# Cross-attention with a gate: score and weight transposes on VectorE, an earlier softmax, and another order of the attention products

## The chip, the cores and the metric

One core of a Trainium2 chip runs the kernel. The time is device microseconds of one execution, median of three runs; less is better. PE is TensorE's matmul row, PEld its weight loads, DVE is VectorE, ACT is ScalarE, POOL is GpSimd, SP issues most of the DMAs.

## What is computed

Everything is float32. Eight batches of 1024 tokens with 1024 features attend to 64 memory rows of 512 features each.

```python
memory_proj = jnp.einsum('bme,de->bmd', memory, W_mem)
scores = jnp.einsum('bnd,bmd->bnm', hidden_states, memory_proj) / jnp.sqrt(jnp.float32(D))
attn = jax.nn.softmax(scores, axis=-1)
memory_context = jnp.einsum('bnm,bmd->bnd', attn, memory_proj)
gate_input = jnp.concatenate([hidden_states, memory_context], axis=-1)
gate = jax.nn.sigmoid(jnp.einsum('bnf,df->bnd', gate_input, W_gate) + b_gate)
fused = hidden_states + gate * memory_context
return _rmsnorm(fused, norm_w)
```

## The kernel before

The tokens are worked on in 16 quads of 512 (four tiles of 128, `t` = 0 to 3). After a setup that multiplies the memory rows by both weight matrices, the large product of a quad is x times the first half of `W_gate`. It is done by Strassen's scheme in two levels: seven outer blocks a quad, in the order 1, 6, 7, 5, 4, 2, 3, and seven inner products each. An inner product is two matmuls over K in the program, four records on PE, and is called a **slot**: 49 slots a quad, slot 0 being the first product of block 1.

`outer_product` issues one block. Its products write four PSUM banks: `af` (its first half by R11 at the block's first slot, its second half by R22 at the sixth, its first half again by R21 at the seventh), `b` (kB, second slot), `c` (kC, third), and `ed` (fourth and fifth). Banks `af` and `ed` come in two sets that alternate by block; `b` and `c` are used again in every block. ACT copies the first half of `af` to `p1` (L901). DVE adds: `u2` = p1 + kB, `u3` = u2 + kC, `u4` = u2 + half of `ed`. POOL adds u3 and u4 to blocks of the output tiles `gate` (`pre`), DVE adds the whole banks (`fin_ed`, `fin_af`), and POOL also makes the left operands of the next block (`inner_s`, tile `l`).

After kC of blocks 4 and 3 come the **visits** (`visit`, L820), the products of the attention weights with the projected memory: for block 5 with 4, and for block 2 with 3. A visit puts the context into its own bank `pc` from rows 0 to 63 of the weights, and the gate's share of the memory into `af` or `ed` from rows 64 to 127, in 64x64 pieces. Before, the earlier block (5 or 2) goes first, with banks `b` and `c` as its `pc`; its sums are held back until then.

The order is written by hand. `plan` puts each step into the list of a slot (`at`), or beside a block (`mid`); `step` runs the list of a slot before its product is issued, in the order in which the entries were put there. The engines keep that program order: each has one queue. The steps that matter here, with t0 the quad's first slot:

- Scores of the next quad run on PE right after the visits of block 3 (`scores`, banks `af` and `ed` of the set that block 2 has just left); ACT copies, DVE adds (`add_scores`, slot 46). They come out with memory rows on partitions (`sT`).
- `transpose_scores` (slot 9) turns them on PE; `softmax_a` (slot 10) takes the maximum on DVE and four exponentials on ACT; `softmax_b` (slot 13) scales; `transpose_attn` (slot 18) turns them back on PE, and four ACT copies lay them out as `attnT`; `attn_difference` follows at slot 22. The visits are at slots 30 and 44.
- `square` of the quad before: tiles 2 and 3 at slots 3 and 4, tiles 0 and 1 at slots 22 and 23; the second of each pair ends with a Sqrt on ACT. `norm` multiplies on DVE and stores; for tiles 2 and 3 at slots 8, 10, 15 and 17, the first beginning with a reciprocal of the Sqrt's result.
- `outer_s` (sums of x blocks, DVE) at slots 3 and 11; `transpose_x` of the next quad at slots 20, 21, 23, 25, 37, 38, 42 and beside block 3.
- `gate` puts a sigmoid on ACT and, a slot or two later, the product with `pc` on DVE (`gated`).

Of the kernel before, what the change touches and what calls it, by code (L numbers as in the profile page):

```python
# [15 lines left out]
P = 128  # L16
# [4 lines left out]
def tile_gated_cross_attention_rmsnorm(  # L21
# [53 lines left out]
    NPAIR = BM // P  # L75
    SCALE = 1.0 / float(D) ** 0.5
    Q4 = D // 4

    const = ctx.enter_context(tc.tile_pool(name="const", bufs=1))
    gpool = ctx.enter_context(tc.tile_pool(name="gpool", bufs=7))  # L80
# [10 lines left out]
    def mm(o, lhsT, rhs, start, stop):  # L91
        pin(nc.tensor.matmul(o, lhsT, rhs, start=start, stop=stop, skip_group_check=True))  # L92

    def tt(eng, o, a, b, op):
        pin(eng.tensor_tensor(o, a, b, op))  # L95
# [4 lines left out]
    def t4k(pool, shape, tag, name):  # L100
        return pool.tile(shape, F32, tag=tag, name=name)
# [234 lines left out]


    A, S, L2, O = {}, {}, {}, {}
    sTs, attns, attnTs, scs, dens, mps, mgs = {}, {}, {}, {}, {}, {}, {}
    def where(q, t=0):  # L340
        return q // QPB, (q % QPB) * QT + t * P

# [79 lines left out]
        tt(nc.vector, flat, flat, part, ALU.add)  # L422
        sTs[q] = sT

    def transpose_scores(q):
        sc = ps_ctx.tile([P, 4, M], F32, tag="ctx", name=f"sc{q}")
        sT = sTs.pop(q)
        for t in range(2):
            pin(
                nc.tensor.transpose(  # L430
                    sc[:, 2 * t : 2 * t + 2, :].rearrange("p r m -> p (r m)"), sT[:, t, :], ident
                )
            )
        scs[q] = sc

    def softmax_a(q):
        sc = scs.pop(q)
        mx = t4k(small, [P, 4], "mx", f"mx{q}")
        pin(nc.vector.tensor_reduce(mx, sc, AX.X, ALU.max))
        pin(nc.scalar.activation(mx, mx, AF.Copy, scale=-SCALE))  # L440
        e = attns[q] = t4k(small, [P, 4, M], "e", f"e{q}")
        den = dens[q] = t4k(small, [P, 4], "den", f"den{q}")
        for t in range(4):
            pin(
                nc.scalar.activation(
                    e[:, t], sc[:, t], AF.Exp, bias=mx[:, t : t + 1], scale=SCALE, accum_out=den[:, t : t + 1]
                )
            )

    def softmax_b(q):  # L450
        e, den = attns[q], dens.pop(q)
        pin(nc.vector.reciprocal(den, den))
        for t in range(4):
            pin(nc.scalar.activation(e[:, t], e[:, t], AF.Copy, scale=den[:, t : t + 1]))

    def transpose_attn(q):
        attn = attns.pop(q)
        pa = ps_ctx.tile([P, 2, P], F32, tag="ctx", name=f"pa{q}")
        for t in range(2):
            pin(  # L460
                nc.tensor.transpose(  # L461
                    pa[:, t, :],
                    attn[:, 2 * t : 2 * t + 2, :].rearrange("p r m -> p (r m)"),
                    ident,
                )
            )

        at = attnTs[q] = t4k(small, [P, 8, P], "attnT", f"attnT{q}")
        for g in (1, 0):
            for r in range(2):  # L470
                pin(
                    nc.scalar.copy(
                        at[g * M : (g + 1) * M, 2 * r : 2 * r + 2, :], pa[r * M : (r + 1) * M]
                    )
                )

    def attn_difference(q):
        at = attnTs[q]
        tt(nc.vector, at[M:P, 4:6, :], at[M:P, 0:2, :], at[M:P, 2:4, :], ALU.subtract)
        tt(nc.vector, at[M:P, 6:8, :], at[M:P, 2:6:2, :], at[M:P, 3:6:2, :], ALU.subtract)  # L480

    def load_mp(b):
        mps[b] = t4k(small, [P, KD, M], "mpb", f"mpb{b}")
# [142 lines left out]
    def plan(q):  # L626
        t0 = SLOTS * q
        nxt = q + 1 < NQ
        for i, o in enumerate(ORDER):
            for part, t in ((0, 1), (1, 2)):  # L630
                if i + 1 < len(ORDER):
                    at(t0 + 7 * i + t, inner_s, q, ORDER[i + 1], part)
                elif nxt:
                    at(t0 + 7 * i + t, inner_s, q + 1, ORDER[0], part)
        if q == 0:
            at(t0 + 7, scores, q)
            at(t0 + 8, add_scores, q)
# [179 lines left out]
    sets = 0  # L817
    held = {}

    def visit(q, o, pcs, af, ed):  # L820

        row, h, g = EXT[o]
        at_, mg = attnTs[q], mgs[q // QPB]
        second = o in SECOND
        for r, k in ((0, af), (1, ed)):
            cols = slice(h * H, (h + 1) * H)
            for t in TOKENS:
                mm(pcs[r][t, :], at_[0:M, 2 * row + r, t], mg[0:M, cols], True, True)
            if second and r == 0:
                for n, left in ((0, g + r), (1, NEG[o])):  # L830
                    part = mg[M:P, h * H + n * C : h * H + (n + 1) * C]
                    for t in TOKENS:
                        mm(k[t, n], at_[M:P, left, t], part, False, True)
            else:
                whole = k.rearrange("p n c -> p (n c)")
                for t in TOKENS:
                    mm(whole[t, :], at_[M:P, g + r, t], mg[M:P, cols], second, True)

    def pre(q, o, u3, u4):

# [39 lines left out]
    def outer_product(q, o):  # L880
# [146 lines left out]
```

## Time and profile before

| | |
|---|---|
| median of three runs | 953.83 us (953.53 to 953.95) |
| the profiled execution's span | 951.8 us |
| PE busy | 939.9 us, 99% |
| DVE busy | 806.5 us, 85% |
| POOL busy | 711.0 us, 75% |
| ACT busy | 361.9 us, 38% |
| granted TensorE clock, mean | 0.997 |

How to read the lines that follow. A row of a timeline has the start in microseconds from the span's start, the duration, the engine, the line of the kernel, the operation, what it writes and reads with the shape, and how many were merged; in brackets the idle time before it and what ended that. A line can be a helper's: all matmuls are at L92, all sums of two tensors at L95. A row of a group has total busy time, mean nanoseconds of one, and idle time before. Matmuls are pipelined: the end of one is modelled, and the next starts before it; what a product takes is read from one start to the next.

### The profile page before, as it was taken

How to read it: one execution, taken by the hardware profiler on the slowest of the kernel's cores; microseconds unless marked ns; L12 is line 12 of the kernel's file. 1: busy time of each engine (PE TensorE's matmuls, PEld its weight loads, DVE VectorE, ACT ScalarE, POOL GpSimd, SP SyncE). 2: the span in 40 equal slices, each digit the busy share in tenths (PEclk: the TensorE clock that was granted, in tenths of full speed). 3: DMA queues.
4: the chain of work that ended last, by engine and by line, in shares of the span. 5: the costliest groups of instructions: out<-in, count | busy, mean ns of one | idle time of the engine just before them, and what ended most of it. 6: DMA issues, size and time to landing. Idle time of an engine off the chain costs nothing.

```text
span 951.8 us, 15584 instructions
## 1 busy us (share of the span) xinstructions
PE 939.9 (99%) x5624; PEld 732.1 (77%) x5624; DVE 806.5 (85%) x1258; ACT 361.9 (38%) x782; POOL 711.0 (75%) x780
## 2 busy tenths in 40 slices
PE   9999999999999999999999999999999999999995
PEld 8546778787877778787877778687877778787773
DVE  6988888888888888888888888888888888888887
ACT  3001235162433525153443526253443526243456
POOL 5997877688676777787686867777686767877683
PEclk9999999999999999999999999999999999999998
DMA  9956664482919365481918366391918466390632
GB/s 377 285 144 161 105 122 112 108 181 48 206 46 185 98 130 131 103 185 39 217 45 174 93 141 138 90 199 32 215 53 166 101 133 144 79 210 25 144 142 89
DMA packets 70923, 128.40 MB, mean 135 GB/s; under 512 B 12352, under 2 KB 49216, under 8 KB 70592
## 3 DMA queue, kind: packets, MB, share of 16 engines
q1 hardware_dynamic: 61664, 93.86, 37.5%
q0 software_dynamic: 9184, 33.56, 19.4%
q8 instruction: 45, 0.74, 0.3%
q14 instruction: 30, 0.25, 0.1%
HBM read 87.56 MB, written 41.68 MB: 136 GB/s over the span
## 4 chain that ended last, share of the span: by engine, by line
PE 97%; DVE 2%; ACT 1%; issue 0%; DVEq 0%
PE af L92 31%; PE ed L92 21%; PE pc L92 10%; PE kC L92 10%; PE kB L92 10%; PE pg L92 5%; PE psT_af L92 5%; PE pm L92 3%; DVE gate L95 1%; PE psT_ed L92 0%; PE pz L92 0%; DVE gate L788 0%; PE sc L430 0%; PE pa L461 0%; PE psT_b L92 0%; PE pt L193 0%
## 5 line engine op out<-in xcount | busy, mean ns | idle before, releaser
L95 POOL TENSOR_TENSOR gate<-gate,u 128x512 f32<-128x512 f32 (+1 forms) x224 | 236.9, 1070 | 187.4 <-DVE u L95 151.3
L685 ACT ACTIVATE gate<-gate 128x512 f32<-128x512 f32 x128 | 80.2, 630 | 225.0 <-DVE gate L95 225.0
L352 DVE STREAM_TRANSPOSE a<-xq 128x512 f32<-128x512 f32 x128 | 141.5, 1108 | 3.4 <-issue 3.4
L95 POOL TENSOR_TENSOR l<-a 128x256 f32<-128x256 f32 x128 | 110.9, 866 | 18.6 <-PE af L92 17.5
L714 DVE SCALAR_TENSOR_TENSOR gate<-gate,ss,nw_sb 128x512 f32<-128x512 f32 x120 | 119.4, 995 | 1.1
L92 PE MATMUL pc<-mg,attnT 64*64 64x512 f32 x512 | 116.8, 595 | 0.1
L92 PE MATMUL ed<-it,l 128*128 128x256 f32 x448 | 115.0, 379 | 0.0
L92 PE MATMUL kB<-it,l 128*128 128x256 f32 x448 | 115.0, 379 | 0.0
L95 DVE TENSOR_TENSOR gate<-gate,pc 128x512 f32<-128x512 f32 x128 | 86.1, 682 | 31.7 <-ACT gate L685 31.7
L901 ACT COPY u<-af 128x256 f32<-128x256 f32 x112 | 40.7, 363 | 182.6 <-PE af L92 182.6
L92 PE MATMUL af<-w,a 128*128 128x256 f32 x384 | 98.5, 379 | 0.0
L92 PEld LDWEIGHTS kB<-it,l 128*128 128x128 f32 x448 | 85.1, 190 | 11.6
L95 DVE TENSOR_TENSOR gate<-gate,ed 128x512 f32<-128x512 f32 x112 | 76.1, 679 | 19.1 <-POOL gate L95 17.5
L92 PEld LDWEIGHTS ed<-it,l 128*128 128x128 f32 x448 | 83.9, 190 | 10.7
L95 DVE TENSOR_TENSOR gate<-gate,af 128x512 f32<-128x512 f32 (+1 forms) x128 | 76.7, 609 | 12.8 <-PE af L92 11.2
L92 PEld LDWEIGHTS af<-w,a 128*128 128x128 f32 x384 | 73.0, 190 | 10.3 <-issue 0.5
L95 POOL TENSOR_TENSOR l<-s 128x256 f32<-128x256 f32 x96 | 78.2, 814 | 3.3 <-DVE it L95 3.3
L92 PEld LDWEIGHTS pc<-mg,attnT 64*64 64x64 f32 x512 | 32.9, 132 | 50.1 <-issue 23.5
L92 PE MATMUL af<-mg,attnT 64*64 64x256 f32 (+1 forms) x384 | 67.4, 456 | 0.0
L92 PE MATMUL ed<-it,a 128*128 128x256 f32 x256 | 67.4, 386 | 0.0
L95 DVE TENSOR_TENSOR u<-u,kC 128x256 f32<-128x256 f32 x112 | 45.9, 410 | 23.8 <-PE kC L92 20.3
L92 PE MATMUL af<-t,s 128*128 128x256 f32 x256 | 65.8, 379 | 0.0
(147 smaller groups left out, 2044.6 us busy)
## 6 DMA issues: line engine op xcount, KB each, us to landing
xq<-in_x SPq DMA_DIRECT2D x64, 512.0 KB, 10.3
gate<-in_x POOLq DMA_DIRECT2D x60, 512.0 KB, 8.4
out<-gate SPq DMA_DIRECT2D x60, 512.0 KB, 3.3
w<-in_w_gate_t SPq DMA_DIRECT2D x8, 512.0 KB, 10.2
w<-in_w_gate_t SPq DMA_DIRECT2D x2, 2048.0 KB, 17.2
mg<-mgd SPq DMA_DIRECT2D x16, 256.0 KB, 5.2
wm<-in_w_mem_t SPq DMA_DIRECT2D x4, 512.0 KB, 6.0
mpd<-mpT SPq DMA_DIRECT2D x4, 512.0 KB, 8.6
```

The source lines that it names most:

```text
L92: pin(nc.tensor.matmul(o, lhsT, rhs, start=start, stop=stop, skip_group_check=True))
L95: pin(eng.tensor_tensor(o, a, b, op))
L352: nc.vector.transpose(A[key][:, :, r * P : (r + 1) * P], chunks(xq[q][:, 4 * t : 4 * t + 4, :], KD)[:, half * KH : (half + 1) * KH],)
L685: pin(nc.scalar.activation(g, g, AF.Sigmoid))
L714: nc.vector.scalar_tensor_tensor(g[:, cols], g[:, cols], rstd[:, t % 2 : t % 2 + 1], nw_sb[:, cols], ALU.mult, ALU.mult,)
L901: pin(nc.scalar.copy(p1, af[:, 0]))
```

## The change

Four things are changed.

1. `turn_scores` and `turn_attn` turn scores and weights on DVE, in blocks of 32x32, where PE did it. With such blocks a token's 64 scores lie on two groups of 32 partitions, so the maximum and the sum of a token are each joined from two halves: `other_half` copies the other group's numbers over with four small ACT copies. There are eight exponentials and eight scalings of 32 columns, in two parts of four, where there were four and four of 64. `attnT` is filled by one DVE transpose and two ACT copies, its upper half in another order (`upper`).
2. The softmax's slots. From quad 1 on: turn and maximum at slot 0, exponentials at 3 and 9, scalings at 13 and 16, turning back at 19, differences at 22. In quad 0: 9, 11, 16, 19, 23, 25, 27.
3. The visits: later block's first half, the earlier block's two halves, later block's second half.
4. One x transpose moves from slot 42 to behind `u3` of block 3, ahead of the earlier block's sums.

```diff
+    def turn_scores(q):
+        sT = sTs.pop(q)
+        sc = scs[q] = t4k(small, [P, 2 * P // B32, B32], "sc", f"sc{q}")
+        pin(nc.vector.transpose(sc.rearrange("p n m -> p (n m)"), sT.rearrange("p t c -> p (t c)")))
+        mx = mxs[q] = t4k(small, [P, 2, 8], "mx", f"mx{q}")
+        pin(nc.vector.tensor_reduce(mx[:, 0], sc, AX.X, ALU.max))
+    def other_half(o, i):
+        for g in range(4):
+            pin(nc.scalar.copy(o[g * B32 : (g + 1) * B32], i[(g ^ 1) * B32 : ((g ^ 1) + 1) * B32]))
+    def softmax_max(q):
+        mx = mxs[q]
+        other_half(mx[:, 1], mx[:, 0])
+    def softmax_exp(q, part):
+        sc, mx = scs[q], mxs[q]
+        if part == 0:
+            dens[q] = t4k(small, [P, 2, 8], "den", f"den{q}")
+            tt(nc.vector, mx[:, 0], mx[:, 0], mx[:, 1], ALU.max)
+            pin(nc.scalar.activation(mx[:, 0], mx[:, 0], AF.Copy, scale=-SCALE))
+        for n in range(4 * part, 4 * part + 4):
             pin(
                 nc.scalar.activation(
...
+                    bias=mx[:, 0, n : n + 1],
+                    scale=SCALE,
+                    accum_out=dens[q][:, 0, n : n + 1],
                 )
             )
+        if part == 1:
+            del mxs[q]
+            other_half(dens[q][:, 1], dens[q][:, 0])
+    def softmax_scale(q, part):
+        sc, den = scs[q], dens[q]
+        if part == 0:
+            tt(nc.vector, den[:, 0], den[:, 0], den[:, 1], ALU.add)
+            pin(nc.vector.reciprocal(den[:, 0], den[:, 0]))
+        for n in range(4 * part, 4 * part + 4):
+            pin(nc.scalar.activation(sc[:, n], sc[:, n], AF.Copy, scale=den[:, 0, n : n + 1]))
+    def turn_attn(q):
+        sc = scs.pop(q)
+        at = attnTs[q] = t4k(small, [P, 8, P], "attnT", f"attnT{q}")
+        pin(
+            nc.vector.transpose(
+                at[:, 0:2].rearrange("p t c -> p (t c)"), sc.rearrange("p n m -> p (n m)")
+            )
+        )
+        for g in (1, 0):
             pin(
+                nc.scalar.copy(
+                    at[g * M : (g + 1) * M, 2:4, :], at[(1 - g) * M : (2 - g) * M, 0:2, :]
                 )
             )
...
-        at(t0 + 9, transpose_scores, q)
-        at(t0 + 10, softmax_a, q)
-        at(t0 + 13, softmax_b, q)
-        at(t0 + 18, transpose_attn, q)
-        at(t0 + 22, attn_difference, q)
+        when = (9, 11, 16, 19, 23, 25, 27) if q == 0 else (0, 3, 9, 13, 16, 19, 22)
+        at(t0 + when[0], turn_scores, q)
+        at(t0 + when[0], softmax_max, q)
+        for part in range(2):
+            at(t0 + when[1 + part], softmax_exp, q, part)
+            at(t0 + when[3 + part], softmax_scale, q, part)
+        at(t0 + when[5], turn_attn, q)
+        at(t0 + when[6], attn_difference, q)
...
-            (20, 0, 0), (21, 1, 0), (23, 2, 0), (25, 3, 0), (37, 2, 1), (38, 3, 1), (42, 0, 1)
+            (20, 0, 0), (21, 1, 0), (23, 2, 0), (25, 3, 0), (37, 2, 1), (38, 3, 1)
         ):
             at(t0 + i, transpose_x, q + 1, t, half)
+        mid((q, 3, 0), transpose_x, q + 1, 0, 1)
...
-            visit(q, f, fp, faf, fed)
             pcs = [ps_ctx.tile([P, H], F32, tag="ctx", name=f"pc{q}_{o}_{r}") for r in range(2)]
-            visit(q, o, pcs, af, ed)
+            visit(q, o, 0, pcs[0], af)
+            visit(q, f, 0, fp[0], faf)
+            visit(q, f, 1, fp[1], fed)
+            visit(q, o, 1, pcs[1], ed)
```

More of the change, by code (lines that the diff above doesn't have):

```diff
@@ L77, in tile_gated_cross_attention_rmsnorm @@
     Q4 = D // 4
+    B32 = 32
     const = ctx.enter_context(tc.tile_pool(name="const", bufs=1))
@@ L338, in tile_gated_cross_attention_rmsnorm @@
     A, S, L2, O = {}, {}, {}, {}
-    sTs, attns, attnTs, scs, dens, mps, mgs = {}, {}, {}, {}, {}, {}, {}
+    sTs, attnTs, scs, mxs, dens, mps, mgs = {}, {}, {}, {}, {}, {}, {}
     def where(q, t=0):
@@ L423, in add_scores @@
         sTs[q] = sT
-    def transpose_scores(q):
-        sc = ps_ctx.tile([P, 4, M], F32, tag="ctx", name=f"sc{q}")
+    def turn_scores(q):
         sT = sTs.pop(q)
-        for t in range(2):
-            pin(
-                nc.tensor.transpose(
-                    sc[:, 2 * t : 2 * t + 2, :].rearrange("p r m -> p (r m)"), sT[:, t, :], ident
-                )
-            )
-        scs[q] = sc
-    def softmax_a(q):
-        sc = scs.pop(q)
[L438 to L443, printed above, removed]
-            pin(
-                nc.scalar.activation(
-                    e[:, t], sc[:, t], AF.Exp, bias=mx[:, t : t + 1], scale=SCALE, accum_out=den[:, t : t + 1]
-                )
-            )
@@ L450, in softmax_b @@
[L450 to L475, printed above, removed]
+        sc = scs[q] = t4k(small, [P, 2 * P // B32, B32], "sc", f"sc{q}")
@@ new lines, in turn_scores @@
+        pin(nc.vector.transpose(sc.rearrange("p n m -> p (n m)"), sT.rearrange("p t c -> p (t c)")))
[14 more added lines that the diff above has]
+        for n in range(4 * part, 4 * part + 4):
+            pin(
+                nc.scalar.activation(
+                    sc[:, n],
+                    sc[:, n],
+                    AF.Exp,
+                    bias=mx[:, 0, n : n + 1],
+                    scale=SCALE,
+                    accum_out=dens[q][:, 0, n : n + 1],
+                )
+            )
+        if part == 1:
+            del mxs[q]
+            other_half(dens[q][:, 1], dens[q][:, 0])
@@ L477, in attn_difference, with upper @@
+    def upper(left):
+        return left ^ 2 if left < 4 else left
     def attn_difference(q):
         at = attnTs[q]
-        tt(nc.vector, at[M:P, 4:6, :], at[M:P, 0:2, :], at[M:P, 2:4, :], ALU.subtract)
-        tt(nc.vector, at[M:P, 6:8, :], at[M:P, 2:6:2, :], at[M:P, 3:6:2, :], ALU.subtract)
+        tt(nc.vector, at[M:P, 4:6, :], at[M:P, 2:4, :], at[M:P, 0:2, :], ALU.subtract)
+        tt(nc.vector, at[M:P, 6:8, :], at[M:P, 0:5:4, :], at[M:P, 1:6:4, :], ALU.subtract)
     def load_mp(b):
@@ L818, in tile_gated_cross_attention_rmsnorm, with visit @@
     held = {}
-    def visit(q, o, pcs, af, ed):
+    def visit(q, o, r, pc, k):
         row, h, g = EXT[o]
@@ L824, in visit @@
         second = o in SECOND
-        for r, k in ((0, af), (1, ed)):
-            cols = slice(h * H, (h + 1) * H)
-            for t in TOKENS:
[L828 to L837, printed above, removed]
+        cols = slice(h * H, (h + 1) * H)
+        for t in TOKENS:
+            mm(pc[t, :], at_[0:M, 2 * row + r, t], mg[0:M, cols], True, True)
+        if second and r == 0:
+            for n, left in ((0, g + r), (1, NEG[o])):
+                part = mg[M:P, h * H + n * C : h * H + (n + 1) * C]
+                for t in TOKENS:
+                    mm(k[t, n], at_[M:P, upper(left), t], part, False, True)
+        else:
+            whole = k.rearrange("p n c -> p (n c)")
+            for t in TOKENS:
+                mm(whole[t, :], at_[M:P, upper(g + r), t], mg[M:P, cols], second, True)
     def pre(q, o, u3, u4):
```

## The prediction

> **What bounds the kernel now.** I read the page first, then the engines' timelines of one quad in the middle of the run (400 to 462 us), because the work of quads 1 to 15 repeats: in the chain in order of time, the same twelve matmuls at the end of a quad start 53.79 us apart.
>
> ```profile
> 404.83 2.59 PE af L92 x12
> ```
> ```profile
> 458.62 2.59 PE af L92 x12
> ```
>
> ```profile
> span 951.8 us, 15584 instructions
> ```
> ```profile
> PE 939.9 (99%) x5624; PEld 732.1 (77%) x5624; DVE 806.5 (85%) x1258; ACT 361.9 (38%) x782; POOL 711.0 (75%) x780
> ```
> ```profile
> PE 97%; DVE 2%; ACT 1%; issue 0%; DVEq 0%
> ```
>
> The reader is to see that the end is set by PE alone: busy for 99% of the span and 97% of the chain that ended last. An instruction on DVE, ACT or POOL costs nothing until PE waits for it, and an instruction taken off PE is worth exactly its place in PE's row. So two questions decide: how much leaves PE, and whether the longer softmax makes PE wait.
>
> **What leaves PE.** Four 128x128 transposes a quad, in two pairs:
>
> ```profile
> 414.16 0.38 PE L430 MATMUL sc<-ident,sT 128*128 128x128 f32 x2
> 414.38 1.03 PE L92 MATMUL kC<-t,l 128*128 128x256 f32 x4
> ```
> ```profile
> 422.15 0.38 PE L461 MATMUL pa<-ident,e 128*128 128x128 f32 x2
> 422.37 1.03 PE L92 MATMUL ed<-it,l 128*128 128x256 f32 x4
> 423.24 1.03 PE L92 MATMUL af<-w,l 128*128 128x256 f32 x4
> ```
>
> The next product starts 0.22 us after each pair; a product (one slot) takes 0.87. Nothing of the 0.22 lies beside other PE work, so 16 quads x 0.44 = **7.0 us saved**.
>
> **What the new order does to ACT and DVE.** The squares of the quad before stand at slots 3 and 4, and the second ends in a Sqrt. The new schedule puts the first four exponentials at slot 3. The list of slot 3 holds the first square already, and slot 4 the second, so ACT's order becomes: square, scale of the maximum, four Exp, square, Sqrt. Only then comes slot 7's copy p1 of `af`. Behind the Sqrt stands more: DVE's reciprocal and norm at slot 8, ahead of everything else in DVE's queue. I follow one quad by its rows.
>
> DVE to the maximum:
>
> ```profile
> 407.19 0.68 DVE L95 TENSOR_TENSOR gate<-gate,af 128x512 f32<-128x512 f32 x1
> ```
> ```profile
> 409.17 0.41 DVE L95 TENSOR_TENSOR u<-u,kB 128x256 f32<-128x256 f32 x1
> ```
> ```profile
> 410.02 1.22 DVE L95 TENSOR_TENSOR a<-a,a 128x1024 f32<-128x1024 f32 x1
> ```
> ```profile
> L352 DVE STREAM_TRANSPOSE a<-xq 128x512 f32<-128x512 f32 x128 | 141.5, 1108 | 3.4 <-issue 3.4
> ```
> ```profile
> L440 ACT ACTIVATE mx<-mx 128x4 f32<-128x4 f32 x16 | 3.3, 206 | 47.7 <-DVE mx L439 47.7
> ```
>
> These are the nearest rows for what is new. ACT's small copy of 32 rows has none of its own. The bounds are 0.10 us (two of them overlapped) and the 0.21 of this row; I take 0.15, the middle, and 0.6 for four. DVE's 128x256 transpose has none either: half of 1.11 is 0.55, all of it (a fixed cost) 1.11; I take 0.57, as DVE's sums above and below grow with the elements (0.41 for 256, 0.68 for 512, 1.22 for 1024). From 407.87: transpose to 408.4, maximum over eight 32-blocks to 408.7 (about the 0.42 of the reduce it replaces), ACT's four copies to 409.3, p1 of slot 0 to 409.65, then u2, u3 (0.34 each back to back) and the 1.22 sum to 411.55, joint maximum to **411.7**. These sit in DVE's idle time and delay nothing yet.
>
> ACT from there:
>
> ```profile
> 409.87 1.06 ACT L699 ACTIVATE junk<-gate 128x1024 f32<-128x1024 f32 x1
> 410.84 0.19 ACT L699 ACTIVATION_READ_ACCUMULATOR junk<-gate 128x1 f32 x1
> 411.04 1.28 ACT L704 ACT_TABLE_LOAD   x1
> 412.33 0.30 ACT L704 ACTIVATE ss<-ss,eps_sb 128x2 f32<-128x2 f32 x1
> 413.50 0.37 ACT L901 COPY u<-af 128x256 f32<-128x256 f32 x1 [0.87 <-PE af L92]
> ```
> ```profile
> 417.12 1.28 ACT L445 ACT_TABLE_LOAD   x1
> 418.42 0.31 ACT L445 ACTIVATE e<-sc,mx 128x64 f32<-128x64 f32 x1
> ```
> ```profile
> 419.95 1.06 ACT L454 ACTIVATE e<-e,den 128x64 f32<-128x64 f32 x4 [0.24 <-DVE den L452]
> ```
>
> Scale 0.2, table 1.30 (417.12 to 418.42), four exponentials 1.1 (now 1.29 for four of twice the width, 418.42 to 419.71; bounds 0.8 and 1.3), square with its read 1.17 (409.87 to 411.04), table 1.29, Sqrt 0.30: Sqrt ends at **417.1** instead of 412.63, and p1 of slot 7 at 417.45 instead of 413.87. Now PE:
>
> ```profile
> 416.97 1.03 PE L92 MATMUL af<-t,l 128*128 128x256 f32 x4
> ```
>
> This product of slot 12 writes the other half of the bank that p1 reads. Without the transposes it is due at 416.75. If the whole bank is waited for, it starts at 417.45: **a new wait of 0.70 us**. Nothing in this trace shows whether the half or the bank counts; I take the bank, since both halves are one tile.
>
> DVE meanwhile stands at the reciprocal:
>
> ```profile
> 413.31 0.16 DVE L710 RECIPROCAL ss<-ss 128x2 f32<-128x2 f32 x1
> 413.50 1.09 DVE L714 SCALAR_TENSOR_TENSOR gate<-gate,ss,nw_sb 128x512 f32<-128x512 f32 x1
> 414.51 0.41 DVE L95 TENSOR_TENSOR u<-u,kB 128x256 f32<-128x256 f32 x1
> ```
> ```profile
> 415.79 0.75 DVE L714 SCALAR_TENSOR_TENSOR gate<-gate,ss,nw_sb 128x512 f32<-128x512 f32 x1
> 416.45 0.42 DVE L439 TENSOR_REDUCE mx<-sc 128x4 f32<-128x256 f32 x1
> 416.78 1.97 DVE L95 TENSOR_TENSOR s<-a,s 128x1024 f32<-128x1024 f32 x1
> 418.67 0.41 DVE L95 TENSOR_TENSOR u<-u,ed 128x256 f32<-128x256 f32 x1
> ```
>
> Its reciprocal moves from 413.31 to 417.15, 3.8 us. Queued behind: norm 1.0, u2 and u3 0.7, norm 0.7 to 0.9, the 1.9 sum, u4 and the `ed` sum 0.95, the new add and the reciprocal of the weights' sums 0.3: 422.75. ACT's scalings of slot 13 wait for that; four at 0.22 (now 0.26 for twice the width, 1.06 for four) and p1 of slot 14 end at 423.97. PE's slot 19 (423.24 above, less 0.44, plus 0.70 = 423.50) writes that bank: **a second wait of 0.47**. The second exponentials, their copies and a third table load fall in ACT's idle time here.
>
> DVE stays late. Its `u2` and `u3` of slots 22 and 23 free the banks of PE's slots 29 and 30:
>
> ```profile
> 429.32 0.42 DVE L95 TENSOR_TENSOR u<-u,kB 128x256 f32<-128x256 f32 x1
> ```
> ```profile
> 430.68 0.38 DVE L95 TENSOR_TENSOR u<-u,kC 128x256 f32<-128x256 f32 x1
> ```
> ```profile
> 431.87 1.03 PE L92 MATMUL kB<-it,l 128*128 128x256 f32 x4
> 432.74 1.03 PE L92 MATMUL kC<-t,l 128*128 128x256 f32 x4
> ```
>
> u4 of slot 11 moves from 418.67 to 421.8, 3.1 us. POOL's sums follow it, and DVE's `ed` sum of the next block follows POOL's. If that lateness of 2.6 to 3.1, with 0.5 for the transpose back, is still there, u2 ends up to 432.9 and u3 up to 434.2, where PE is due at 431.87 - 0.44 + 1.17 = 432.60 and 0.87 later: **up to 0.7 more** in two waits; nothing, if DVE catches up 1 us. I take 0.2, near the lower end, because the norm of 1.09 above is longer than its group and PE's own delay gives DVE room.
>
> **The visits.** The same products in another order, without one more or less.
>
> ```profile
> 448.62 1.03 PE L92 MATMUL kC<-w,l 128*128 128x256 f32 x4
> 449.57 0.65 PE L92 MATMUL pc<-mg,attnT 64*64 64x512 f32 x2
> ```
> ```profile
> 451.59 0.69 DVE L95 TENSOR_TENSOR gate<-gate,ed 128x512 f32<-128x512 f32 x1
> ```
> ```profile
> 453.08 0.38 PE L92 MATMUL psT_ed<-a,mpb 64*64 64x256 f32 x2
> ```
>
> The entry costs 0.95 where a slot is 0.87. At most 0.09 x 32 = 2.9 us could go, as the first bank is no longer one that DVE has just read; nothing, if the change to 64x64 itself costs it. I take nothing. On the other side the earlier block's `ed` ends one group (0.86) later, so its sum runs 452.45 to 453.14, and the next scores, whose bank it frees, come **0.1 late**. The 1.1 us x transpose moved from slot 42 to just ahead of these sums fits in the group's 0.86 and the idle time there.
>
> DMA: no step issues one. Output stores on SP follow norms 3 to 4 us late; SP's next loads are a slot list away, and a landing takes
>
> ```profile
> out<-gate SPq DMA_DIRECT2D x60, 512.0 KB, 3.3
> ```
>
> 3.3 us, so the first store's tile is free at about 424, and POOL's next use of such a tile, behind u4's sum, moves by the same 3 us. I cost that at nothing; uncovered, it would be up to 1 us a quad.
>
> **Sum.** Quads 1 to 15: 0.70 + 0.47 + 0.2 + 0.1 = 1.47 each, 22.0 us. Less 7.0: **+15 us**, span 951.8 to 966.8. Around the span lie 2.0 us (the runs' median 953.83 less 951.8), so 968.8. Quad 0 has no squares ahead and its own later slots; I give it no wait.
>
> **Tables.** In ACT's rows above a load takes 1.30 from its start to the next instruction, and the square's read ends 0.01 ahead of it.
>
> The Trainium skill, "ScalarE: Activation LUTs", section "What ACT_TABLE_LOAD costs", says that every switch to another set costs about 2.66 us, the load and a drain of 1.38. By that rule the time would be about 1010, and the rows, which leave no room for a drain, disagree.
>
> The mechanism as a rival: if each of the two switches ahead of p1 cost its 1.30 twice, the first wait would grow by 2.6, 15 x 2.6 = 39 us: 1008. Only a delay hidden in these rows could bring it. Chance 0.02.
>
> **Rivals.** (1) Not slower: ACT's chain arrives in time. The place is PE's slot 12; it decides at 0.70 us, when Sqrt ends by 416.4. With small copies at 0.10, exponentials at 0.20, scalings at 0.18, and DVE's first two steps 0.13 shorter, the chain is 0.63 shorter and the first wait 0.07. If the norms also take the 0.75 of 415.79 instead of 1.09, the second goes too. All waits gone gives 953.8 - 7.0 = **946.8** (to 944 with the visits' entry). For it: ACT is idle 62%; against: the two tables, square, Sqrt and p1, 4.4 us of the 5.75 after the maximum, have firm rows. Chance 0.23. In between, waits of about 0.45 a quad eat the saving: 954, chance 0.09. (2) DVE becomes the bound: if a 128x256 transpose costs the 1.11 of the wide one, the first wait is 1.23 and the two of slots 29 and 30 the full 0.7: 15 x 2.5 - 7.0 = +30, **984**. Against: DVE has 15% left. Chance 0.06.
>
> **How the numbers follow.** My forecast, waits of 0.75 to 2.3 us a quad (958 to 981 us), has 0.60. With rival 2 and the 1008 case that is 0.68 for slower by over 0.2% (about the 2 us that runs of this kernel can tell apart), 0.09 within, 0.23 faster. The range runs from rival 1's full saving to just past rival 2: 946 to 985. The half of rival 1 that also gains at the visits, and 1008, are outside. If only the half bank counts, the first wait moves to slot 13 and vanishes, but then PE is earlier at slots 20, 29 and 30 and waits there for p1, u2 and u3: 0.3 and the full 0.7, in place of 1.37. That is 963, inside the forecast.
>
> **What would show it.** PE rows of slots 12 and 19 starting late with a wait on ACT's p1; five table loads a quad, not four; DVE's reciprocal of slot 8 waiting 3 to 4 us for the Sqrt; scores 0.1 late behind the `ed` sum. It is wrong if PE keeps its 0.87 through slots 7 to 31: then the quad's period is 53.35 and the saving stands whole.

## The result and the profile after

The changed kernel takes 1012.28 us (1011.90 to 1013.42, four runs) beside 953.89 us for the kernel before on the same chip: 1.0614 of it, 95% interval 1.0599 to 1.0629. The forecast was slower, 968.8 us; the loss is 58 us where 15 were forecast, and the time lies above the range.

The page of the changed kernel, its busy times and the chain that ended last:

```profile
PE 951.3 (94%) x5560; PEld 725.8 (72%) x5560; DVE 836.0 (83%) x1322; ACT 427.2 (42%) x1085; POOL 698.6 (69%) x780
...
DVE 38%; PE 23%; POOL 14%; ACT 13%; issue 11%; DVEq 0%; POOLq 0%; ACTq 0%
```

PE is no longer the bound. It held 97% of the chain and holds 23%; no other engine is full, DVE is even less busy by share than before. A chain that runs over four engines while none is full says that they wait for each other in turn. The granted clock is 0.997 as before, so the time was lost in waits, not in slower matmuls.

The chain of the changed kernel in order of time, around slot 40 of two quads that follow each other:

```profile
404.76 1.24 POOL gate L96
...
406.03 0.69 DVE gate L96
406.72 0.73 DVE gate L732
...
407.85 1.28 DVE gate L96 x2
...
409.15 0.63 ACT gate L703
409.78 0.27 ACT u L918
```

The same product starts at 410.19 (right behind the last `u` row) and at 467.89: a quad takes 57.70 us, before 53.79. So 3.91 us are lost in each of quads 1 to 15, 58.6 us in all, and one quad explains the whole result. PE's timeline of that quad has these late starts, each with the row ahead of it (in brackets the idle time and what ended it):

```profile
435.02 1.03 PE L93 MATMUL ed<-it,l 128*128 128x256 f32 x4
437.81 1.10 PE L93 MATMUL af<-t,l 128*128 128x256 f32 x4 [1.76 <-ACT u L918]
438.75 1.03 PE L93 MATMUL af<-t,s 128*128 128x256 f32 x4
...
443.06 1.03 PE L93 MATMUL ed<-it,l 128*128 128x256 f32 x4
444.96 1.10 PE L93 MATMUL af<-w,l 128*128 128x256 f32 x4 [0.87 <-ACT u L918]
...
453.67 1.03 PE L93 MATMUL kB<-it,l 128*128 128x256 f32 x4
454.87 1.10 PE L93 MATMUL kC<-t,l 128*128 128x256 f32 x4 [0.17 <-DVE u L96]
...
466.51 1.03 PE L93 MATMUL ed<-it,l 128*128 128x256 f32 x4
467.89 1.10 PE L93 MATMUL af<-w,l 128*128 128x256 f32 x4 [0.35 <-ACT u L918]
```

A start is late by what it lies beyond the start before it plus 0.864 us, the time of a slot to three digits. The product behind a wait begins 0.94 instead of 0.864 later (437.81 to 438.75), so each wait also costs 0.08 in the next slot. Slot 5 has the 0.08 alone: it starts at 429.77, the next product at 430.71.

| place | forecast, us a quad | measured |
|---|---|---|
| transposes off PE | -0.44 | -0.44 |
| slot 12, behind p1 of slot 7 | 0.70 | 1.93 + 0.08 |
| slot 19, behind p1 of slot 14 | 0.47 | 1.04 + 0.08 |
| slot 30, behind u3 | 0.2 | 0.34 + 0.08 |
| slot 40, behind p1 of slot 35 | none | 0.52 + 0.08 |
| slot 5 | none | 0.08 |
| scores after the visits | 0.1 | 0.16 |
| sum | 1.03 | 3.95 |

The sum is 0.04 above the 3.91 of the period. The waits listed by who waits for whom, over the whole run of the changed kernel (total us, times, longest):

```profile
DVE ss L728 <- ACT ss L722: 60.6, 16, 4.0
...
PE af L93 <- ACT u L918: 44.0, 44, 2.1
```

These are two of the signs named beforehand: PE waits for ACT's p1 about three times a quad (44 in 15 quads), and DVE's reciprocal waits 4.0 us for the Sqrt. The others came too: ACT loads a table five times a quad (30 loads for the exponentials, 30 for the Sqrt and 17 for the sigmoid in the run), and the scores are late. The stores, which the prediction costed at nothing, have no share of the chain: POOL waits for a landing seven times in the run, at most 1.6 us, and the chain doesn't go through these waits.

### The profile page after: what moved, and what is told of

It is laid out like the page before. It is cut to its first block, busy times and chain, and to the rows that moved or that the text cites. A ratio compares the mean times of both kernels' runs of the same rounds, so it can differ in the third digit from the quotient of the medians.

```text
span 1010.5 us, 15808 instructions
## 1 busy us (share of the span) xinstructions
PE 951.3 (94%) x5560; PEld 725.8 (72%) x5560; DVE 836.0 (83%) x1322; ACT 427.2 (42%) x1085; POOL 698.6 (69%) x780
## 4 chain that ended last, share of the span: by engine, by line
DVE 38%; PE 23%; POOL 14%; ACT 13%; issue 11%; DVEq 0%; POOLq 0%; ACTq 0%
DVE gate L96 10%; POOL gate L96 10%; DVE gate L732 7%; PE af L93 6%; DVE u L96 6%; DVE s L96 5%; PE pg L93 5%; POOL l L96 5%; DVE a L353 4%; PE pc L93 4%; PE pm L93 2%; ACT L722 2%; ACT gate L703 2%; ACT sc L451 2%; ACT L451 2%
## 5 line engine op out<-in xcount | busy, mean ns | idle before, releaser
L96 POOL TENSOR_TENSOR gate<-gate,u 128x512 f32<-128x512 f32 (+1 forms) x224 | 241.9, 1094 | 252.3 <-DVE u L96 174.4
L732 DVE SCALAR_TENSOR_TENSOR gate<-gate,ss,nw_sb 128x512 f32<-128x512 f32 x120 | 127.9, 1066 | 1.1
L96 POOL TENSOR_TENSOR l<-a 128x256 f32<-128x256 f32 x128 | 106.1, 829 | 24.5 <-DVE mx L96 23.2
L93 PE MATMUL af<-w,l 128*128 128x256 f32 x256 | 69.0, 392 | 17.8 <-ACT u L918 17.8
L93 PE MATMUL af<-t,l 128*128 128x256 f32 x192 | 50.4, 385 | 26.2 <-ACT u L918 26.2
L93 PEld LDWEIGHTS af<-w,l 128*128 128x128 f32 x256 | 45.0, 189 | 36.2 <-POOL l L96 28.5
```

What stands on the lines that cost most here:

```text
L732: nc.vector.scalar_tensor_tensor(g[:, cols], g[:, cols], rstd[:, t % 2 : t % 2 + 1], nw_sb[:, cols], ALU.mult, ALU.mult,)
```

## The experiments

The leading theory throughout is one of order: p1, which PE needs, stands in ACT's queue behind steps of the softmax and of the norm. The rivals are the new work itself: the third table load, DVE's transposes and the small copies, the new order of the visits. Where an expectation has a letter, it stands for a variant that it spells out. Times a quad are taken from start to start of the same product. "Slots" means the tuple `when` of quads 1 to 15: turn, exponentials in two parts, scalings in two parts, turning back, differences.

### Order alone, on the kernel before

```diff
-        at(t0 + 9, transpose_scores, q)
-        at(t0 + 10, softmax_a, q)
+        at(t0 + (3 if q else 9), transpose_scores, q)
+        at(t0 + (3 if q else 10), softmax_a, q)
```

> The kernel before, transposes on TensorE and the old visits, with only the score transposes and the maximum with its four exponentials moved from slots 9 and 10 to slot 3 in quads 1 to 15, so that they stand between the two squares. Theory A: Sqrt ends near 5 us later, p1 of slot 7 comes after slot 12 is due, VectorE's reciprocal waits 4 to 5 us: 1.2 to 3 us a quad, 972 to 1000 us, without any of the new work. Theory B and C: 954 to 960 us (some 0.3 us a quad for the transposes' bank at slot 3).

Measured: 996.17 us, 1.0444 (1.0428 to 1.0459), 56.58 a quad. With PE's own transposes, no new instruction and one table load a quad fewer (three instead of four), moving the score transposes, the maximum and the exponentials to slot 3 loses 42 us. PE's timeline of this kernel at slot 12 and at the transposes back:

```profile
431.52 1.10 PE L92 MATMUL af<-t,l 128*128 128x256 f32 x4 [0.83 <-ACT u L901]
...
435.91 1.03 PE L92 MATMUL ed<-it,a 128*128 128x256 f32 x4
437.51 0.33 PE L461 MATMUL pa<-ident,e 128*128 128x128 f32 x1 [0.58 <-ACT e L454]
...
438.16 1.03 PE L92 MATMUL ed<-it,l 128*128 128x256 f32 x4
```

Slot 12 is 1.01 late with the same releaser as in the changed kernel. The two transposes back wait for the scalings, 1.17 together (435.91 to 438.16 is 2.25, where the same two products lie 1.08 apart before), because on DVE the reciprocal of the weights' sums stands behind the norms, and these behind the late Sqrt. The two entries to the visits take another 0.55. Order is enough for a loss of this size.

### The exponential's table taken away

```diff
-                    AF.Exp,
+                    AF.Square,
```

> The changed kernel with Square in place of Exp in the softmax (the exponential is left out), which needs no table of its own: same instructions, same slots, two table loads a quad less. Theory A: one load of 1.3 us less ahead of Sqrt and p1, so PE's wait at slot 12 falls from 2.0 to 0.7 us, the one at slot 19 stays near 1 us: 20 us less, 985 to 997 us. Theory B and C: within 6 us of 1012.

Measured: 992.92 us, 1.0416 (1.0401 to 1.0432), 56.41 a quad. Three of five table loads a quad go (both for the exponentials, and one for a Sqrt behind them), and 19 of the 58 us. The exponential is left out in this kernel. Slot 12 is 0.65 late instead of 1.93; slot 19 stays at 1.03 and slot 40 at 0.51. So the tables are a third of the loss. One of the three loads stood ahead of p1 of slot 7, and slot 12's wait fell by 1.28, the length of one load; the other two bring nothing that shows, as slots 19 and 40 are as late as before.

### The first exponentials one slot later

```diff
-... else (0, 3, 9, 13, 16, 19, 22)
+... else (0, 4, 9, 13, 16, 19, 22)
```

> The changed kernel with one number changed: the first four exponentials of quads 1 to 15 at slot 4 instead of 3, so that they stand behind the second square and its Sqrt, not between the squares. Theory A (order on ACT): what holds PE is the Exp table load, four exponentials and the load back for Sqrt, placed ahead of VectorE's reciprocal of slot 8. Then the 4 us wait of that reciprocal falls under 1 us and PE's waits at slots 19, 30 and 40 go; p1 of slot 7 is still behind both loads, so 0 to 0.8 us a quad may stay at slot 12: 948 to 960 us. Theory B (amount of work: two more transposes on VectorE, 28 more small instructions on ACT): the work is the same, so 1000 to 1012 us. Theory C (the visits' order and the moved x transpose make the quad's end late): the same 1000 to 1012 us.

Measured: 986.81 us, 1.0348 (1.0333 to 1.0364), 55.96 a quad: 25 us better, with one table load a quad fewer, but far from the 948 to 960 that were expected. The Sqrt is no longer behind the exponentials, p1 of slot 7 still is: it stands behind two table loads. Slot 12 is 0.84 late, slot 19 0.44, slot 30 0.32, slot 40 0.50. The 0.84 is about the most that I had allowed there, and the reciprocal's wait went as expected, to 0.2; but I took the other waits to go with it. DVE now waits 1.96 us for the same p1 at its `u2`, and what stands behind that stays late.

### All exponentials behind p1

```diff
-... else (0, 3, 9, 13, 16, 19, 22)
+... else (0, 9, 9, 13, 16, 19, 22)
```

> The changed kernel with all eight exponentials at slot 9 in quads 1 to 15: behind p1 of slot 7, one Exp table load a quad less. Theory A: neither the Sqrt nor p1 of slot 7 stands behind an Exp any more, PE's wait at slot 12 goes wholly and the others with it: 946 to 951 us, a little under the run with slot 4. Theory B: 1000 to 1012 us less at most 5 for the load. Theory C: 1000 to 1012 us.

Measured: 963.22 us, 1.0103 (1.0086 to 1.012), 54.41 a quad. One move of four exponentials takes back 49 of the 58 us, with every new instruction still there but one table load a quad; slot 12's wait is gone and the reciprocal waits 0.3. The missing load alone can't account for that: without three of them the kernel above gained 19 us. The time lies above the 946 to 951 that were expected, as slot 40 is still 0.50 late, slot 19 0.11 and the scores 0.16. PE, ACT, DVE and POOL at slot 40, in this kernel's timelines:

```profile
448.13 1.10 PE L93 MATMUL af<-w,l 128*128 128x256 f32 x4 [0.34 <-ACT u L918]
```
```profile
444.70 0.63 ACT L703 ACTIVATE gate<-gate 128x512 f32<-128x512 f32 x1 [4.00 <-DVE gate L96]
447.10 0.63 ACT L703 ACTIVATE gate<-gate 128x512 f32<-128x512 f32 x1 [1.77 <-DVE gate L96]
447.63 0.35 ACT L918 COPY u<-af 128x256 f32<-128x256 f32 x1
```
```profile
443.98 0.69 DVE L96 TENSOR_TENSOR gate<-gate,ed 128x512 f32<-128x512 f32 x1 [0.32 <-POOL gate L96]
...
446.39 0.68 DVE L96 TENSOR_TENSOR gate<-gate,af 128x512 f32<-128x512 f32 x1
```
```profile
435.06 4.34 POOL L96 TENSOR_TENSOR gate<-gate,u 128x512 f32<-128x512 f32 x4 [2.93 <-DVE u L96]
...
442.68 1.95 POOL L96 TENSOR_TENSOR gate<-gate,u 128x512 f32<-128x512 f32 x2
```

This is a chain of its own. POOL starts at 435.06, when DVE's u3 has come, and then works without a gap past 444; DVE's sum at 443.98 waits for it, a norm and two more sums stand behind that, ACT's sigmoid waits for the last of them, and p1 of slot 35 stands behind the sigmoid though its product, started at 443.31, was done 3 us before. The chain shown for the changed kernel at 404.76 is the same one.

### The visits' order, in both directions

The old order in the kernel just shown (the x transpose back at slot 42 too), and the new order in the kernel before (the x transpose moved with it). The first as a diff; the second is parts 3 and 4 of the change alone:

```diff
+            visit(q, f, 0, fp[0], faf)
+            visit(q, f, 1, fp[1], fed)
             visit(q, o, 0, pcs[0], af)
-            visit(q, f, 0, fp[0], faf)
-            visit(q, f, 1, fp[1], fed)
             visit(q, o, 1, pcs[1], ed)
...
-        mid((q, 3, 0), transpose_x, q + 1, 0, 1)
+        at(t0 + 42, transpose_x, q + 1, 0, 1)
```

> The 963 us run (all exponentials at slot 9) with the visits in their old order and the x transpose back at slot 42. Theory C (the visits' order makes the earlier block's sums and sigmoids late): the 0.58 us at slot 40 goes, 953 to 956 us. Theory A2 (POOL's chain behind u3 of block 5 makes them late): within 3 us of 963.

> The kernel before with only the visits in the new order and the x transpose behind u3 of block 3 instead of at slot 42. Forecast by the prediction's term: the scores come 0.1 us late a quad and the entry to the visits stays at 0.95 us: 953.5 to 957 us. If the entry shrinks, 951 us. If theory C holds, 960 us or more.

Measured: 963.22 us, 1.0092 (1.0077 to 1.0107) for the first, no difference from the kernel it was made from. Slot 40's wait is gone, but the entry to the visits of slot 30 now takes 1.55 instead of 0.95, with 0.47 of idle time ended by a DVE sum of the `u` row, because the first visit writes bank `b`, which DVE has just read for u2. So the wait has moved more than gone: PE, held up at the entry, no longer comes too early for slot 40.

The second: 960.16 us, 1.0064 (1.0047 to 1.0081), 54.10 a quad, so the new order, with the x transpose that moves with it, costs 6 us alone. That is above the 953.5 to 957 that the prediction's term gave, and at the lower end of the variant that blames the visits: they are a part of the loss. From the second visits' first row to slot 46, in the PE timelines of the kernel before and of this one:

```profile
457.60 1.03 PE L92 MATMUL ed<-it,l 128*128 128x256 f32 x4
```
```profile
452.71 0.65 PE L92 MATMUL pc<-mg,attnT 64*64 64x512 f32 x2
...
460.90 1.03 PE L92 MATMUL ed<-it,l 128*128 128x256 f32 x4
```

Before, 449.57 to 457.60 is 8.03; here 8.19. That is the term of 0.1 for late scores, and it is 0.16. The rest is at slot 40, late by 0.07 to 0.16 and then 0.08 in 11 of 14 quads, and 1.1 us once, in quad 0.

### DVE's turn alone, at the old slots

```diff
-... else (0, 3, 9, 13, 16, 19, 22)
+... else (9, 10, 10, 13, 13, 18, 22)
```

with the old visits and the x transpose at slot 42, as above.

> The changed kernel with part 1 of the change alone: scores and weights turned on VectorE at the old slots (9, 10, 13, 18, 22), all eight exponentials at 10, old visits, x transpose at 42. Theory A: transposes and small instructions in themselves cost little, but VectorE meets the 0.44 us turn, the four copies and the joint maximum in its full stretch of slots 8 to 29: 950 to 963 us. Theory B: the work itself is the loss, 985 us or more.

Measured: 1013.83 us, 1.0625 (1.0608 to 1.0643), 57.74 a quad, 50 us above the range expected for order and inside the one for the work itself (985 us or more). PE's timeline of this kernel at slot 19 of three quads that follow each other, then ACT's in the second of them:

```profile
391.06 1.10 PE L93 MATMUL af<-w,l 128*128 128x256 f32 x4 [2.59 <-ACT u L918]
...
448.92 1.10 PE L93 MATMUL af<-w,l 128*128 128x256 f32 x4 [2.59 <-ACT u L918]
...
505.35 2.04 PE L93 MATMUL af<-w,l 128*128 128x256 f32 x4 [2.65 <-ACT u L918]
507.18 1.66 PE L93 MATMUL af<-w,a 128*128 128x256 f32 x4
508.68 1.03 PE L93 MATMUL af<-t,s 128*128 128x256 f32 x4
```
```profile
439.14 0.81 ACT L437 COPY mx<-mx 32x8 f32<-32x8 f32 x4 [1.89 <-DVE mx L432]
...
446.72 1.80 ACT L470 ACTIVATE sc<-sc,den 128x32 f32<-128x32 f32 x8 [0.53 <-DVE den L468]
448.43 0.35 ACT L918 COPY u<-af 128x256 f32<-128x256 f32 x1
```

The split of a token over two groups of 32 rows makes the softmax a relay between ACT and DVE: 9.4 us from the first copies to the last scaling. At slot 13 all eight scalings stand ahead of p1 of slot 14, and slot 19 is 2.75 late. I had counted the instructions, not the relay.

```diff
-... else (9, 10, 10, 13, 13, 18, 22)
+... else (9, 10, 10, 15, 15, 18, 22)
```

> The 1014 us run e9_dve_turn_alone (VectorE's transposes at the old slots) with the eight scalings at slot 15 instead of 13, so that they stand behind p1 of slot 14 in ACT's queue and not ahead of it. Theory A: the 2.8 us at slot 19 is p1 standing behind the scalings, which wait for a chain of copies from ACT to VectorE and back; behind them it has only the exponentials and copies ahead and ends about 2 us earlier: 975 to 992 us. Theory B (the work itself): 1005 to 1015 us.

Measured: 971.13 us, 1.0183 (1.0169 to 1.0197). The same instructions with the scalings behind p1 are 43 us faster, below the 975 to 992 expected. So most of the loss at the old slots was order and not the work, though not all of the 43 us is the wait (see the last section). At 54.77 a quad 17 us are still lost here: slot 19 is 0.62 late, and the entries to the visits take 0.49 and 0.19 longer than before.

### Room for DVE

Scalings at 15 and 16, the differences after the x transposes, one of these a slot later:

```diff
-... else (0, 3, 9, 13, 16, 19, 22)
+... else (0, 9, 9, 15, 16, 19, 26)
...
-            (20, 0, 0), (21, 1, 0), (23, 2, 0), (25, 3, 0), (37, 2, 1), (38, 3, 1)
+            (20, 0, 0), (21, 1, 0), (24 if q else 23, 2, 0), (25, 3, 0), (37, 2, 1), (38, 3, 1)
```

> Exponentials at slot 9 as in the 963 us run, and three more steps of quads 1 to 15 moved out of the way of p1 and of u3 of block 5: first scalings at slot 15 instead of 13, the x transpose of slot 23 at 24, the weights' differences at 26 instead of 22. Theory A2: what is left of the loss at slot 9 is VectorE reaching u3 of block 5 about 1.3 us later than before, which starts POOL's gapless chain (four gate sums, left operands, gate sum) late, and so the sums, the sigmoids and p1 at slot 40 (0.58 us a quad), and p1 of slot 14 behind the scalings (0.2 us). With the moves both go: the quad is 53.5 us, 947 to 952 us, faster than the kernel before. Theory B (amount of work on VectorE): only where it waits changes: 957 to 965 us.

Measured: 952.99 us (952.63 to 955.12), 0.999 (0.9981 to 0.9999), 53.64 a quad. The waits of slots 12, 19 and 40 are gone, and the time is 1 us above the range expected.

Three more kernels vary it: the old order of visits at both places (the x transpose at slot 42) with differences at 24; the old order at the second visits only, also with differences at 24; and the latter with differences at 26. The diff is that of the last two:

```diff
+            if o == 4:
+                visit(q, o, 0, pcs[0], af)
             visit(q, f, 0, fp[0], faf)
             visit(q, f, 1, fp[1], fed)
+            if o == 3:
+                visit(q, o, 0, pcs[0], af)
             visit(q, o, 1, pcs[1], ed)
```

> The same slots with both visits in the old order and the x transpose at slot 42. The old order asks for banks b and c at once behind kC, so VectorE's lateness stands there as a wait of 0.1 to 0.5 us a visit (0.6 and 0.2 in e7_slot9_old_visits): 948 to 957 us, at or above e10_hybrid. If VectorE is on time at the visits now, it is the same as e10_hybrid.

> As e6_room (exponentials at slot 9, scalings at 15 and 16, the x transpose of slot 23 at 24), with the differences at slot 24 instead of 26 and with the new visits' order only at blocks 5 and 4; blocks 2 and 3 go in the old order, so that the scores' bank comes free a group earlier. Theory A2: in e6_room the quad still loses 0.16 us where the scores wait for the late sum and 0.1 to 0.4 where the visits wait for the differences; both go here: 947 to 950 us, ratio 0.993 to 0.996. Theory B: 952 us or more.

> The whole computation. The changed kernel with softmax slots (0, 9, 9, 15, 16, 19, 26), the x transpose of slot 23 at 24, the new order of visits at blocks 5 and 4 and the old one at blocks 2 and 3. Two runs stand beside it: e6_room (new order at both visits, differences at 26, 53.64 a quad) and e10_hybrid (differences at 24, 53.80 a quad). Theory: TensorE's saving of 0.44 a quad stands in both; what e6_room gives back is 0.16 where the scores wait for the earlier block's sum after the new order at blocks 2 and 3, and 0.08 at its first visits; what e10_hybrid gives back is 0.41 at its first visits, since the differences at slot 24 stand ahead of two x transposes, u4, u2 and u3 of block 4. With both removed 0.08 a quad is left: a period of 53.45 to 53.5, 950 to 951 us, 0.996 to 0.998 of before. Rival: the old order at blocks 2 and 3 brings its own entry wait back once DVE's order before it is that of e6_room (late u3 as in e7_slot9_old_visits, 0.2 a quad); then 953 to 956.

Measured, in this order: 964.73 us, 1.0117 (1.0103 to 1.0131); 956.11 us, 1.0027 (1.0017 to 1.0037); and 951.62 us (951.35 to 952.96, nine runs), 0.9976 (0.9966 to 0.9986). The first two are slower than forecast, the first by 8 us and the second by 6; the last is inside its range as a ratio and 0.6 us above it as a time. PE's timelines give a typical quad in four pieces, from start to start; the first of the three kernels is not in the table:

| us | before | new order twice, 26 | old second, 24 | old second, 26 |
|---|---|---|---|---|
| slot 46 to first visits | 29.89 | 29.45 | 29.45 | 29.45 |
| first visits to slot 32 | 4.57 | 4.65 | 4.98 | 4.67 |
| slot 32 to second visits | 11.31 | 11.31 | 11.32 | 11.32 |
| second visits to slot 46 | 8.03 | 8.19 | 8.02 | 8.02 |
| quad | 53.80 | 53.60 | 53.77 | 53.46 |

The first row is the saving of 0.44 in full: nothing waits there any more. What was given back stands in the other rows: 0.16 for scores behind the new order at the second visits, and at the first visits 0.1 with the differences at 26, 0.4 with them at 24. With 24 the differences stand ahead of two x transposes, and bank `b`, which the second of the visits' four groups writes, isn't free in time. PE's timeline with 24:

```profile
435.39 0.65 PE L93 MATMUL pc<-mg,attnT 64*64 64x512 f32 x2 [0.18 <-DVE u L96]
```

With the old order at both places and 24, that entry takes 1.92 instead of 0.96; no run has the old order there with 26.

So the change holds a gain, of 2.3 us against the kernel before, if its softmax stands where ACT and DVE have room and the new order of visits is kept for the first visits only. The mean period is 53.51, 0.28 less than before, or 4.0 us over 14 periods. The last quad gives 2.0 of them back: there slot 26 waits for a p1 and loses 0.81, and the two visits take 0.78 and 0.83 longer, less the 0.44 saved.

## Why the prediction was wrong

Its mechanism was right: PE waits at slots 12 and 19 for a p1 that stands behind the softmax, DVE's reciprocal behind the Sqrt, five table loads a quad. Two steps failed. The terms of slots 12 and 19 were too small, 1.17 where 3.13 came, as the chain that they hang on was begun at DVE's time in the kernel before and its small instructions were taken too short. And the wait at slot 40, 0.60, was left out.

**The term of slot 12**, 0.70, measured 1.93. ACT's timeline of the changed kernel around it:

```profile
428.41 0.81 ACT L437 COPY mx<-mx 32x8 f32<-32x8 f32 x4 [0.18 <-DVE mx L432]
429.25 0.37 ACT L918 COPY u<-af 128x256 f32<-128x256 f32 x1
...
431.91 0.21 ACT L448 ACTIVATE mx<-mx 128x8 f32<-128x8 f32 x1 [1.11 <-DVE mx L96]
432.13 1.28 ACT L451 ACT_TABLE_LOAD   x1
433.43 0.32 ACT L451 ACTIVATE sc<-sc,mx 128x32 f32<-128x32 f32 x1
...
434.67 1.04 ACT L717 ACTIVATE junk<-gate 128x1024 f32<-128x1024 f32 x1
...
435.81 1.28 ACT L722 ACT_TABLE_LOAD   x1
437.11 0.30 ACT L722 ACTIVATE ss<-ss,eps_sb 128x2 f32<-128x2 f32 x1
437.31 0.35 ACT L918 COPY u<-af 128x256 f32<-128x256 f32 x1
```

And DVE's:

```profile
426.89 0.68 DVE L96 TENSOR_TENSOR gate<-gate,af 128x512 f32<-128x512 f32 x1
427.49 0.44 DVE L430 STREAM_TRANSPOSE sc<-sT 128x256 f32<-128x256 f32 x1
...
437.44 0.17 DVE L728 RECIPROCAL ss<-ss 128x2 f32<-128x2 f32 x1 [4.03 <-ACT ss L722]
...
439.83 2.29 DVE L96 TENSOR_TENSOR s<-a,s 128x1024 f32<-128x1024 f32 x1
```

Laid over each other at slot 0 (406.39 before, 425.45 after, 19.06 apart), the steps of the forecast drift like this:

| step | forecast | after, less 19.06 | late by |
|---|---|---|---|
| DVE starts the turn | 407.87 | 408.43 | 0.56 |
| p1 of slot 0 done | 409.65 | 410.56 | 0.91 |
| joint maximum | 411.7 | 412.75 | 1.05 |
| first Exp | 413.2 | 414.37 | 1.17 |
| four Exp done | 414.3 | 415.61 | 1.31 |
| Sqrt done | 417.1 | 418.35 | 1.25 |
| PE's slot 12 starts | 417.45 | 418.75 | 1.30 |

Nearly half of the error is ahead of the first step: I took the start from DVE's row in the kernel before, but in the changed one DVE comes to slot 0 late, by 0.64 in the row at 426.89 (407.19 before). That comes from the visits. The prediction had the earlier block's `ed` sum one group later and followed it to the scores only, for 0.1; but DVE works on from that sum (417.55) with 0.69 us of idle time up to the turn, so all that stands behind it is late too. The kernel before with the new order of visits alone is as late at slot 0. (The new softmax with the old visits is 0.50 late there: a sum of x blocks at the quad's end takes 2.29 instead of 1.21, and why it does is open.) The next 0.35 is mostly the four small copies, 0.81 us instead of 0.6, and the 0.18 before them. The Trainium skill, "ScalarE: Activation LUTs", section "What ACT_TABLE_LOAD costs", says that such an ACTIVATE takes 186 ns plus 0.833 ns a column, 0.19 us for 8 columns as an estimate; the trace agrees with 0.20 each, above my middle of 0.15. Four exponentials of half the width take 1.24 us up to the next instruction (433.43 to 434.67), those of full width took 1.29: I had let the width count for 0.05 each. No single number of these is large; a wait is what is left after slack, so each of them counts whole. The last 0.15 is the step from the end of p1 to PE's start, for which the forecast had nothing.

**Rival 1 fell**: Sqrt, which would have had to end 0.7 earlier than forecast, ended 1.25 later. DVE's transpose, the unknown on which I spent a rival, took 0.44 us, less than the 0.57 taken and far from 1.11. **Rival 2 fell.** The third rival fell too: 432.13 to 433.43 is one load of 1.28 and 0.02, and without one load slot 12's wait fell by 1.28 and not by more. That its 1008 lies near the measured 1012 is chance.

**Half or bank**, left open, is settled for this kernel: slot 12 writes the half that p1 doesn't read, and it starts 0.15 after p1 ends at 437.66. PE's wait is one for ACT in the program's order, so it doesn't show what the chip would do without it. The Trainium skill, "PSUM — Partial Sum Buffer", section "PSUM bank collisions raise a hardware error", says that accesses of two engines are to be kept apart by bank and group of 32 partitions, not by address; the wait in the trace agrees with it. Read beforehand, that sentence would have spoken for the bank.

**The term of slot 19**, 0.47, measured 1.04. PE was due there 1.36 later than forecast, and p1 ended 1.8 later, as the relay over DVE (reciprocal, norms, the `outer_s` sum of 2.29 instead of 1.97, then the weights' sums) began with the later Sqrt.

**Slots 29 and 30**, taken as 0.2 within 0 to 0.7: 0.42 at slot 30. The reason for the low value, that DVE would catch up, did not hold.

**Slot 40 was not in the sum at all**, 0.60 a quad, 9 us. I followed DVE's lateness up to slots 29 and 30 and stopped, noting only that POOL's sums follow. But POOL then works without a gap, and its lateness returns through DVE's sums, the sigmoid and p1. The rows of the kernel in which the other waits were small show it (0.50 late, 963 us), and it went when DVE was given room. A part of it belongs to the visits: their new order alone makes slot 40 late by 0.07 to 0.16.

**The saving on PE** was right, 0.44 a quad (29.89 to 29.45), and so was taking no gain at the visits' entry, which stays at 0.95; the late scores were 0.16, not 0.1.

**The range** failed with these: its terms were treated as if they could err each by itself, but the waits hang on one chain, and a start 0.56 late moves all that come behind it.

## What to carry to other kernels

When a step is put earlier in an in-order queue, look for the next instruction behind it that the bound engine needs, here a 0.35 us copy, and put the step behind that one: this one move, and the table load that it spared, was worth 49 of 58 us. A softmax that goes back and forth between two engines costs its whole relay time to what stands behind it, not the sum of its instructions. Follow a late engine through every consumer until a gap absorbs it, with the times of the changed kernel and not of the old one, and expect the waits to err together.

## What the hardware showed besides

In the kernel with DVE's turn at the old slots, each of the 15 stops at slot 19 lasts 2.5 to 2.65 us, and after 14 of them the granted TensorE clock falls to half. Its windows (the clock is the number ahead of the last two columns):

```profile
505.30:507.20 1.90, 1.85 (x5) 1.53 (x6) 1.80 (x5) 0.00 (x0) 0.89 (x1) 0.50 0.00 0
...
448.90:450.70 1.80, 1.78 (x8) 1.62 (x9) 1.70 (x4) 0.00 (x0) 0.81 (x1) 1.00 0.00 0
```

In PE's rows of this kernel above, the two products from 505.35 on take 1.83 and 1.50 us instead of 0.86. The quad from 391.06 to 448.92, with the drop, takes 57.86 us, the one from 448.92, the only stop without it, 56.43: 1.43 us each, 20 us over the run, nearly half of the 43 us that the move of the scalings saved. The kernel's mean clock is 0.973 to 0.974 and that of all others 0.994 to 0.997.

The trace shows when a stop counts. The 14 slow stretches last 3.41 us each and begin 17 times 3.41 apart, at 160.30, 218.32 and so on to 392.40, and, on the same grid, at 505.04 to 969.26, while the stops come every 57.86. So the clock seems to be set over windows of 3.41 us that don't move with the program. In the window ahead of each slow stretch PE is idle for at least 2.1 us (the least is from 388.98 to 392.40); in the one that holds most of the stop that escaped, 447.02 to 450.43, for 1.9. That fits a bound on the idle time in one window, between these two.

The changed kernel's own stops, 1.76 us and once 2.11, leave the clock alone:

```profile
437.80:440.50 2.70, 2.69 (x13) 2.39 (x14) 2.60 (x5) 2.66 (x10) 1.12 (x1) 1.00 1.06 213
```

The Trainium skill, "TensorE: Matmul & The Clock Gate", part 1, says that the clock is halved after an idle window of about 3.4 us that runs freely, and its table in "Why this matters for your kernels" warns of gaps above about 3 us. Here 2.1 us of idle time in a window were enough, so these figures are too high for this kernel; the fixed grid, and the one stop of the same length that escaped, agree with a window that runs freely.
